# Laying the buffer pools of two graph layers over each other, and reloading a layer's values from another queue

## The chip, the cores and the metric

The kernel runs on one core of a Trainium2 chip. Its time is the device time of one launch in microseconds (us). A core has five engines with an instruction stream each: PE (TensorE), DVE (VectorE), ACT (ScalarE), POOL (GpSimd) and SP (SyncE, which here only issues DMAs). Each works through its stream in order; semaphores tie the streams together. Data lies in SBUF (128 partitions), matmul results in PSUM, everything else in DRAM.

## The reference

A graph of N = 2708 nodes with 256 features, and a sparse weighted adjacency matrix. Two residual layers, each followed by a layer norm:

```python
# layer 0, two steps
R = S + eye(N); R = R / R.sum(-1, keepdims=True)
Xf = Xa = X; Z = 0
for n in range(2):
    A = top_p_attention(Xa, W1, W2, W3)     # softmax rows, the largest entries up to 0.9 of the mass
    Xf = R @ Xf
    Xa = A @ Xa
    Z = Z + Xf @ U1[n].T + Xa @ U2[n].T
x = layernorm(x + layernorm(X + Z) * ln_g + ln_b)
# layer 1, four heads of 64
Wh  = einsum('nd,hdo->nho', x, W)
s_i = einsum('nho,ho->nh', Wh, a_src); s_j = einsum('nho,ho->nh', Wh, a_dst)
e   = leaky_relu(s_i[:, None, :] + s_j[None, :, :], 0.2)
e   = where(adj != 0 or i == j, e, -inf)
x   = layernorm(x + einsum('ijh,jho->iho', softmax(e, axis=1), Wh))
```

## The kernel before, in words

The nodes are cut into 22 tiles, 16 of 128 rows and 6 of 110. All arithmetic is in float32.

Layer 0 (`fast_layer0`) runs two steps of 22 attention tiles. For a tile it makes the scores `e` (128 x 2708), finds the kept entries on DVE, transposes `e` in pieces and multiplies it with the node values (`weigh`, tiles `tr`, `eT`, `att`). Beside that runs a second stream of matmuls, the walk with R (tiles `blk`, `walk`), and per tile a chain of small steps written as generators. The last chain, `finish`, adds the terms, takes two layer norms (BN statistics on DVE, `ln_ve` and `ln_rs` on POOL, the scaling on DVE at L906), writes the new features into `xe`, and then calls `sources`. The order inside layer 0 is written out by hand (`slot`, `step`, `doing`, inside `manual_schedule`); what stands outside of it is put in order by the framework's scheduler.

`sources` prepares layer 1 for a tile of nodes: it transposes the features (L141), copies them (`xT`, L143), multiplies them with the layer's weights (L147), and from the product makes on ACT the exponentials `sb` and `tj` (L151, L152), the source score `s_src` (L153) and the values times `sb` (`cs`, L157). The values go to DRAM, to `vd[t]` (L160, on SP's queue).

Layer 1 (`layer1`) takes the target nodes in three groups of 8, 8 and 6 tiles (1024, 1024 and 660 columns) and, for each group, all 22 source tiles `j`. Before a group, `targets` makes `r`, the targets' exponentials spread over all partitions: four transposes (`aux`, L1101) and one ACT exponential (L1105) for each of the group's tiles. For a source tile, `neighbours` loads a block of the adjacency matrix (`bar`, L1115, on SP's queue, four buffers), turns it into a 0/1 mask on ACT (sign L1116, square L1121), and in the blocks that hold the diagonal sets it on POOL in between (L1119, L1120). DVE then makes for each head `pt` = max(r, tj) x mask (L1168), and PE multiplies `pt` with the values `v[j]` (L1176, 8 matmuls of 512 columns) and with `bj[j]`, which is `sb` spread over 32 columns and gives the softmax denominator (L1183, 8 matmuls). The sums stay in six PSUM banks over the 22 source tiles. At the end of a group `settle` turns them back, divides, adds the residual, takes the layer norm and stores.

All the values are read back from DRAM at the start of layer 1, for the 22 tiles one after the other, by ACT's queue, and all `bj` are made there on POOL:

```python
for t in range(NT):
    m = rows[t]
    nc.scalar.dma_start(v[t][:m].rearrange("p h o -> p (h o)"), vd[t][:m])
    nc.gpsimd.tensor_copy(bj[t][:m], sb[:m, t, :].unsqueeze(2).to_broadcast([m, H, 32]))
```

SBUF and PSUM are handed out in pools that lie one after the other in the order in which they are opened. Layer 0 closes its pools before layer 1 opens its own, which therefore come to lie over the same addresses. Nothing makes the engines stop there: an instruction of layer 1 that writes a new tile waits on semaphores until the old users of what lies below have finished. So which pool lies over which decides when the first loads, masks and exponentials of layer 1 can start. In the kernel before, the four `bar` buffers and part of `r` lie over buffers that `finish` uses (`heldp`, `finp`).

After both layers a flag says whether the fast path's assumptions held; if not, `general_layer0` and `layer1` run again. With these inputs they don't.

Of the kernel before, what the change touches and what calls it, by code (L numbers as in the profile page):

```python
# [8 lines left out]
F32 = mybir.dt.float32  # L9
# [5 lines left out]
PSUM = bass.MemoryType.PSUM  # L15

P = 128
# [21 lines left out]
HELD = 8  # L39
# [6 lines left out]
def kernel(  # L46
# [16 lines left out]
    nc = tc.nc  # L63
    N, D = x.shape
    DA = w1T.shape[1]
    STEPS = u1T.shape[0]
    H, _, FO = gat_w.shape
    DC = D // P
    NT = (N + P - 1) // P
# [44 lines left out]
    vd = [kept.tile([P, D], F32, name=f"v_{t}") for t in range(NT)]  # L114
# [339 lines left out]
    def fast_layer0():  # L454

        l0 = ExitStack()
        w0 = l0.enter_context(tc.tile_pool(name="w0", bufs=1))
        rowp = l0.enter_context(tc.tile_pool(name="rowp", bufs=2))
        keep = l0.enter_context(tc.tile_pool(name="keep", bufs=1))
        HN = N // 2  # L460
        HT = NT // 2
        pieces = [(c, min(CHUNK, HN - c)) for c in range(0, HN, CHUNK)]
# [43 lines left out]
        nc.gpsimd.memset(wants, 0.0)  # L506
        nc.gpsimd.memset(haves, 0.0)

        qT = keep.tile([P, N], F32, name="qT")
        yw = keep.tile([P, NT, D], F32, name="yw")  # L510
        ba = keep.tile([P, NT, D], F32, name="ba")
        rinv = keep.tile([P, NT], F32, name="rinv")

        dram = l0.enter_context(tc.tile_pool(name="dram", bufs=1, space=bass.MemoryType.DRAM))
        c1 = [dram.tile([P, D], F32, name=f"c1_{t}") for t in range(NT)]
        c2 = [dram.tile([P, D], F32, name=f"c2_{t}") for t in range(NT)]

        sortp = l0.enter_context(tc.tile_pool(name="sortp", bufs=1))
        heldp = l0.enter_context(tc.tile_pool(name="heldp", bufs=HELD))
        finp = l0.enter_context(tc.tile_pool(name="finp", bufs=2))  # L520
        ep = l0.enter_context(tc.tile_pool(name="ep", bufs=3))
        wk = l0.enter_context(tc.tile_pool(name="wk", bufs=1))

        kT = [wk.tile([P, HN], F32, name="junk"), keep.tile([P, HN], F32, name="kT1")]
        tpp = l0.enter_context(tc.tile_pool(name="tpp", bufs=3))
        adjp = l0.enter_context(tc.tile_pool(name="adjp", bufs=3))
        ps_lg = l0.enter_context(tc.tile_pool(name="ps_lg", bufs=2, space=PSUM))
        ps_tr = l0.enter_context(tc.tile_pool(name="ps_tr", bufs=2, space=PSUM))
        ps_at = l0.enter_context(tc.tile_pool(name="ps_at", bufs=1, space=PSUM))
        ps_wk = l0.enter_context(tc.tile_pool(name="ps_wk", bufs=1, space=PSUM))  # L530


        tmp = ep.tile([P, N], F32, name="e")
# [534 lines left out]

    def layer1():
        l1 = ExitStack()  # L1070
        keep = l1.enter_context(tc.tile_pool(name="keep1", bufs=1))
        pp = l1.enter_context(tc.tile_pool(name="pp", bufs=2))
        GT = 8
        spans = [list(range(g, min(g + GT, NT))) for g in range(0, NT, GT)]
        GW = GT * rows[0]


        v = [keep.tile([P, H, FO], F32, name=f"v{t}") for t in range(NT)]
        bj = [keep.tile([P, H, 32], F32, name=f"bj{t}") for t in range(NT)]
        for t in range(NT):  # L1080
            m = rows[t]
            nc.scalar.dma_start(v[t][:m].rearrange("p h o -> p (h o)"), vd[t][:m])
            nc.gpsimd.tensor_copy(
                bj[t][:m], sb[:m, t, :].unsqueeze(2).to_broadcast([m, H, 32])
            )

        rp = l1.enter_context(tc.tile_pool(name="rp", bufs=2))
        adjp = l1.enter_context(tc.tile_pool(name="adjp1", bufs=4))
        pj = l1.enter_context(tc.tile_pool(name="pj", bufs=2))
        ps_v = l1.enter_context(tc.tile_pool(name="ps_v", bufs=1, space=PSUM))  # L1090
        ps_u = l1.enter_context(tc.tile_pool(name="ps_u", bufs=2, space=PSUM))

        def targets(g):

            r = rp.tile([P, H, GW], F32, name="r")
            i0 = off[spans[g][0]]
            for t in spans[g]:
                m = rows[t]
                tr = ps_u.tile([P, H, P], F32, name="aux")
                for h in range(H):  # L1100
                    nc.tensor.transpose(  # L1101
                        tr[:, h, :m], s_src[:m, t, h : h + 1].to_broadcast([m, P]),
                        ident[:m, :m],
                    )
                nc.scalar.activation(  # L1105
                    r[:, :, off[t] - i0 : off[t + 1] - i0], tr[:, :, :m], AF.Exp, scale=1.0 - NEG_SLOPE
                )
            return r

        def neighbours(g, j):  # L1110

            k = rows[j]
            i0, i1 = off[spans[g][0]], off[spans[g][-1] + 1]
            bar = adjp.tile([P, GW], F32, name="bar")[:k, : i1 - i0]
            nc.sync.dma_start(bar, adjT[off[j] : off[j + 1], i0:i1])  # L1115
            nc.scalar.activation(bar, bar, AF.Sign)  # L1116
            if j in spans[g]:
                own = bar[:, off[j] - i0 : off[j + 1] - i0]
                nc.gpsimd.tensor_mul(own, own, offdiag[:k, :k])  # L1119
                nc.gpsimd.tensor_add(own, own, ident[:k, :k])  # L1120
            nc.scalar.activation(bar, bar, AF.Square)  # L1121
            return bar
# [27 lines left out]
        for g, span in enumerate(spans):  # L1150
            gw = off[span[-1] + 1] - off[span[0]]
            cuts = [(c, min(CHUNK, gw - c)) for c in range(0, gw, CHUNK)]
            acc = [
                [ps_v.tile([P, CHUNK], F32, name=f"acc{k}_{c}") for c in range(len(cuts))]
                for k in range(3)
            ]
            for j in range(NT):
                k = rows[j]
                if j == 2 and due:
                    settle(*due)  # L1160
                if j == NT // 2 and g + 1 < len(spans):
                    r_next = targets(g + 1)
                mask = neighbours(g, j)
                at = dict(start=(j == 0), stop=(j == NT - 1), skip_group_check=True)
                pts = []
                for h in range(H):
                    pt = pj.tile([P, GW], F32, name=f"pt{h}")
                    nc.vector.scalar_tensor_tensor(  # L1168
                        pt[:k, :gw], r[:k, h, :gw], tj[:k, j, h : h + 1], mask,
                        op0=ALU.max, op1=ALU.mult,  # L1170
                    )
                    pts.append(pt)
                    if h % 2 == 1:
                        for c, (c0, w) in enumerate(cuts):
                            for q in range(2):
                                nc.tensor.matmul(  # L1176
                                    acc[h // 2][c][q * FO : (q + 1) * FO, :w],
                                    v[j][:k, h - 1 + q, :],
                                    pts[h - 1 + q][:k, c0 : c0 + w], **at,
                                )  # L1180
                for c, (c0, w) in enumerate(cuts):
                    for h in range(H):
                        nc.tensor.matmul(  # L1183
                            acc[2][c][h * 32 : (h + 1) * 32, :w],
                            bj[j][:k, h, :], pts[h][:k, c0 : c0 + w], **at,
                        )
            r = r_next
            val = pp.tile([P, 2, GW], F32, name="val")
            den = pp.tile([P, GW], F32, name="den")
            for c, (c0, w) in enumerate(cuts):  # L1190
                nc.scalar.copy(val[:, 0, c0 : c0 + w], acc[0][c][:, :w])
                nc.vector.tensor_copy(val[:, 1, c0 : c0 + w], acc[1][c][:, :w])
                nc.scalar.copy(den[:, c0 : c0 + w], acc[2][c][:, :w])
            due = (g, val, den)
        settle(*due)
        l1.close()

    fast_layer0()
    layer1()
    flag = nc.values_load(bad[0:1, 0:1])  # L1200
    with tc.If(flag > 0):
        general_layer0()
        layer1()
# [45 lines left out]
```

The softmax here doesn't subtract the row's maximum and nothing guards it: scores larger than these inputs give would overflow.

## Time and profile before

| | |
|---|---|
| time, median of 3 runs | 1722.71 us (1722.70 to 1722.73) |
| span of the profiled execution | 1720.4 us |
| PE busy | 1624.2 us (94%) |
| DVE busy | 1221.5 us (71%) |
| ACT busy | 771.1 us (45%) |
| POOL busy | 450.9 us (26%) |
| moved by DMA | 113.92 MB, mean 66 GB/s |
| end of layer 0's last layer norm to the first matmul of layer 1 | 1314.8 to 1336.2 us |

Busy times are sums over the whole span. "L1168" is line 1168 of the kernel. In the lists of waits, a row says which engine, at which line, stood idle until which other one had finished something, for how long in total, how often, and the longest; where an instruction waits for several others, the row names the one that came last by the profile. In the timelines, instructions of one line that follow each other are merged; "ACTq" and "SPq" are the parts of ACT and SP that issue DMAs.

### The profile page before, as it was taken

How to read it: one execution, taken by the hardware profiler on the slowest of the kernel's cores; microseconds unless marked ns; L12 is line 12 of the kernel's file. 1: busy time of each engine (PE TensorE's matmuls, PEld its weight loads, DVE VectorE, ACT ScalarE, POOL GpSimd, SP SyncE). 2: the span in 40 equal slices, each digit the busy share in tenths (PEclk: the TensorE clock that was granted, in tenths of full speed). 3: DMA queues.
4: the chain of work that ended last, by engine and by line, in shares of the span. 5: the costliest groups of instructions: out<-in, count | busy, mean ns of one | idle time of the engine just before them, and what ended most of it. 6: DMA issues, size and time to landing. Idle time of an engine off the chain costs nothing.

```text
span 1720.4 us, 24503 instructions
## 1 busy us (share of the span) xinstructions
PE 1624.2 (94%) x8434; PEld 1080.7 (63%) x8434; DVE 1221.5 (71%) x3681; ACT 771.1 (45%) x1345; POOL 450.9 (26%) x915
## 2 busy tenths in 40 slices
PE   5799999999999998999999999999995999999895
PEld 4577777777777776777787878777774332322332
DVE  2754555554555108888989999999891979888896
ACT  1233333333333236656676666766632544243241
POOL 0011111111111133322344444345433300440313
PEclk9899999999999999999999999999997999999998
DMA  6111011101111132212222233322213323232231
GB/s 162 33 45 45 26 42 43 42 24 43 42 39 42 41 104 65 62 48 70 78 81 81 68 84 84 84 56 72 73 39 115 95 83 92 86 97 77 73 84 32
DMA packets 153875, 113.92 MB, mean 66 GB/s; under 512 B 39898, under 2 KB 144094, under 8 KB 153742
## 3 DMA queue, kind: packets, MB, share of 16 engines
q1 hardware_dynamic: 145048, 101.88, 21.8%
q10 hardware_dynamic: 6582, 4.84, 1.0%
q0 software_dynamic: 2112, 5.55, 0.9%
q8 instruction: 68, 1.11, 0.3%
q14 instruction: 65, 0.53, 0.1%
HBM read 101.16 MB, written 11.09 MB: 65 GB/s over the span
## 4 chain that ended last, share of the span: by engine, by line
PE 70%; DVE 15%; ACT 6%; POOL 4%; DMA 2%; issue 2%; ACTq 0%; SPq 0%; POOLq 0%; DVEq 0%
PE att L187 20%; PE walk L816 16%; PE acc L1176 11%; PE acc L1183 6%; PE lg L591 4%; PE tr L172 3%; ACT e L595 3%; PE tr L559 2%; DVE cand L696 2%; PE tr L872 2%; PE tr L852 2%; DVE scr L762 2%; DVE e L765 1%; DVE scr L681 1%; DVE work L716 1%
## 5 line engine op out<-in xcount | busy, mean ns | idle before, releaser
L1168 DVE SCALAR_TENSOR_TENSOR pt<-r,tj,bar 128x1024 f32<-128x1024 f32 (+3 forms) x264 | 296.6, 1185 | 49.2 <-DMA v<-v 20.0
L616 ACT ACTIVATE junk<-e,minus,rth 128x2708 bf16<-128x2708 f32 (+1 forms) x88 | 232.8, 2646 | 33.5 <-POOL rth L648 32.7
L816 PE MATMUL walk<-xe,blk 128*128 128x257 f32 (+3 forms) x968 | 243.8, 385 | 0.0
L187 PE MATMUL att<-xe,eT 128*128 128x256 f32 (+3 forms) x968 | 233.4, 381 | 7.6 <-ACT eT L178 7.6
L187 PE MATMUL att<-ba,eT 128*128 128x256 f32 (+3 forms) x968 | 235.2, 384 | 5.0 <-ACT eT L178 5.0
L1176 PE MATMUL acc<-pt,v 128*64 128x512 f32 (+3 forms) x1056 | 229.8, 553 | 4.6 <-DVE pt L1168 4.6
L816 PE MATMUL walk<-yw,blk 128*128 128x256 f32 (+3 forms) x968 | 228.2, 381 | 1.7 <-ACT xw L886 1.7
L178 ACT COPY eT<-tr 128x512 f32<-128x512 f32 (+5 forms) x264 | 136.9, 536 | 193.8 <-PE tr L172 193.4
L816 PEld LDWEIGHTS walk<-xe,blk 128*128 128x128 f32 (+3 forms) x968 | 173.7, 187 | 64.9 <-issue 41.8
L816 PEld LDWEIGHTS walk<-yw,blk 128*128 128x128 f32 (+3 forms) x968 | 176.9, 186 | 42.2 <-issue 12.3
L696 DVE MAX8 cand<-e 128x8 f32<-128x170 f32 (+1 forms) x352 | 89.4, 323 | 146.8 <-ACT e L595 146.8
L187 PEld LDWEIGHTS att<-ba,eT 128*128 128x128 f32 (+3 forms) x968 | 172.6, 188 | 33.4 <-ACT eT L178 10.2
L187 PEld LDWEIGHTS att<-xe,eT 128*128 128x128 f32 (+3 forms) x968 | 171.0, 186 | 35.7 <-ACT eT L178 12.6
L595 ACT ACTIVATE e<-lg 128x1024 f32<-128x1024 f32 (+1 forms) x132 | 121.0, 921 | 133.3 <-PE lg L591 128.4
L1176 PEld LDWEIGHTS acc<-pt,v 128*64 128x64 f32 (+1 forms) x1056 | 73.6, 137 | 153.9 <-issue 110.5
L172 PE MATMUL tr<-ident,e 128*128 128x128 f32 (+3 forms) x968 | 139.0, 270 | 6.1 <-DVE e L765 4.9
L172 PEld LDWEIGHTS tr<-ident,e 128*128 128x128 f32 (+3 forms) x968 | 116.4, 139 | 30.9 <-issue 5.7
L1116 ACT ACTIVATE bar<-bar 128x1024 f32<-128x1024 f32 (+3 forms) x66 | 62.9, 955 | 144.7 <-DMA bar<-in_adjT_dram 127.6
L1183 PE MATMUL acc<-pt,bj 128*32 128x512 f32 (+3 forms) x1056 | 124.6, 549 | 0.0
L829 DVE TENSOR_TENSOR xf<-walk,xe 128x257 f32<-128x257 f32 (+1 forms) x22 | 9.4, 426 | 156.9 <-PE walk L816 156.9
L696 DVE MAX8 cand<-scr 128x8 f32<-128x97 f32 (+1 forms) x616 | 101.7, 244 | 0.0
L714 DVE MAX8 top<-work 128x8 f32<-128x128 f32 (+3 forms) x242 | 82.4, 340 | 8.3
(194 smaller groups left out, 2009.6 us busy)
## 6 DMA issues: line engine op xcount, KB each, us to landing
blk<-in_adjT_dram SPq DMA_DIRECT2D x32, 704.0 KB
bar<-in_adjT_dram SPq DMA_DIRECT2D x32, 512.0 KB
blk<-in_adjT_dram SPq DMA_DIRECT2D x32, 330.0 KB
blk<-in_adjT_dram SPq DMA_DIRECT2D x32, 320.0 KB
blk<-in_adjT_dram SPq DMA_DIRECT2D x12, 605.0 KB
bar<-in_adjT_dram SPq DMA_DIRECT2D x12, 440.0 KB
bar<-in_adjT_dram SPq DMA_DIRECT2D x16, 330.0 KB
c<-cs POOLq DMA_DIRECT2D x32, 128.0 KB, 2.9
```

What stands on the lines that cost most here:

```text
L172: nc.tensor.transpose(tr[: rows[t], q, :m], e[:m, off[t] : off[t + 1]], ident[:m, :m])
L178: copy(eT[:k, : len(grp), :m], tr[:k, : len(grp), :m])
L187: nc.tensor.matmul(acc, eT[: rows[t], q, :m], value(t), start=(t == 0), stop=(t == NT - 1),)
L591: nc.tensor.matmul(lg[:m, h, :w], qT[part, cols], kT[s][part, c0 : c0 + w], start=True, stop=True,)
L595: nc.scalar.activation(halves[:m, :, c0 : c0 + w], lg[:m, :, :w], AF.Exp, accum_out=zp[:m, n : n + 1],)
L616: nc.scalar.activation(junk[:m], e[:m], func, scale=rth, bias=minus1[:m], accum_out=acc)
L696: nc.vector.max(cand[:, n, :], src[:m, n * size : min(N, (n + 1) * size)])
L714: nc.vector.max(top[:, k : k + 8], work if k else flat)
L816: nc.tensor.matmul(ac[:m, :w], blk[: rows[j], j - j0, :m], cur[: rows[j], j, 0:w], start=(j == 0), stop=(j == NT - 1),)
L1168: nc.vector.scalar_tensor_tensor(pt[:k, :gw], r[:k, h, :gw], tj[:k, j, h : h + 1], mask, op0=ALU.max, op1=ALU.mult,)
L1176: nc.tensor.matmul(acc[h // 2][c][q * FO : (q + 1) * FO, :w], v[j][:k, h - 1 + q, :], pts[h - 1 + q][:k, c0 : c0 + w], **at,)
L1183: nc.tensor.matmul(acc[2][c][h * 32 : (h + 1) * 32, :w], bj[j][:k, h, :], pts[h][:k, c0 : c0 + w], **at,)
```

## The change

In both layers all pools are opened together, in another order, so that other pools lie over each other; the number and the size of the buffers stay as they are. In layer 0 the order is now `heldp`, `finp`, `rowp`, `w0`, `keep`, `sortp`, `adjp`, `ep`, `tpp`, `wk`, and in PSUM `ps_lg`, `ps_wk`, `ps_at`, `ps_tr`; in layer 1 it is `pp`, `keep1`, `pj`, `adjp1`, `rp`, and `ps_u`, `ps_v`. By this `pp` (results of a whole group) lies over `heldp`, `finp` and `rowp`; `keep1` (`v`, `bj`, allotted from tile 21 down to tile 0) lies over the last 64 bytes of `rowp`, over `w0` and over part of `keep`; `pj` (`pt`) lies over `keep` (`yw`, `ba`, `qT`); `adjp1` (`bar`) lies over `keep` (`qT`, `kT1`), `sortp` and the first 4 kB of `adjp`; and `rp` (`r`) over `adjp` and `ep`.

The reload of `v[j]` and the making of `bj[j]` move from the start of layer 1 into the loop of the first group: they are called one source tile at a time, ahead of that tile's adjacency load. The load is issued from SP's queue instead of ACT's.

```diff
--- before.py
+++ after.py
@@ -454,9 +454,18 @@
     def fast_layer0():
 
         l0 = ExitStack()
-        w0 = l0.enter_context(tc.tile_pool(name="w0", bufs=1))
-        rowp = l0.enter_context(tc.tile_pool(name="rowp", bufs=2))
-        keep = l0.enter_context(tc.tile_pool(name="keep", bufs=1))
+
+        heldp, finp, rowp, w0, keep, sortp, adjp, ep, tpp, wk = (
+            l0.enter_context(tc.tile_pool(name=name, bufs=bufs))
+            for name, bufs in (
+                ("heldp", HELD), ("finp", 2), ("rowp", 2), ("w0", 1), ("keep", 1),
+                ("sortp", 1), ("adjp", 3), ("ep", 3), ("tpp", 3), ("wk", 1),
+            )
+        )
+        ps_lg, ps_wk, ps_at, ps_tr = (
+            l0.enter_context(tc.tile_pool(name=name, bufs=bufs, space=PSUM))
+            for name, bufs in (("ps_lg", 2), ("ps_wk", 1), ("ps_at", 1), ("ps_tr", 2))
+        )
         HN = N // 2
         HT = NT // 2
         pieces = [(c, min(CHUNK, HN - c)) for c in range(0, HN, CHUNK)]
@@ -506,28 +515,17 @@
         nc.gpsimd.memset(wants, 0.0)
         nc.gpsimd.memset(haves, 0.0)
 
-        qT = keep.tile([P, N], F32, name="qT")
         yw = keep.tile([P, NT, D], F32, name="yw")
         ba = keep.tile([P, NT, D], F32, name="ba")
         rinv = keep.tile([P, NT], F32, name="rinv")
+        qT = keep.tile([P, N], F32, name="qT")
 
         dram = l0.enter_context(tc.tile_pool(name="dram", bufs=1, space=bass.MemoryType.DRAM))
         c1 = [dram.tile([P, D], F32, name=f"c1_{t}") for t in range(NT)]
         c2 = [dram.tile([P, D], F32, name=f"c2_{t}") for t in range(NT)]
 
-        sortp = l0.enter_context(tc.tile_pool(name="sortp", bufs=1))
-        heldp = l0.enter_context(tc.tile_pool(name="heldp", bufs=HELD))
-        finp = l0.enter_context(tc.tile_pool(name="finp", bufs=2))
-        ep = l0.enter_context(tc.tile_pool(name="ep", bufs=3))
-        wk = l0.enter_context(tc.tile_pool(name="wk", bufs=1))
 
         kT = [wk.tile([P, HN], F32, name="junk"), keep.tile([P, HN], F32, name="kT1")]
-        tpp = l0.enter_context(tc.tile_pool(name="tpp", bufs=3))
-        adjp = l0.enter_context(tc.tile_pool(name="adjp", bufs=3))
-        ps_lg = l0.enter_context(tc.tile_pool(name="ps_lg", bufs=2, space=PSUM))
-        ps_tr = l0.enter_context(tc.tile_pool(name="ps_tr", bufs=2, space=PSUM))
-        ps_at = l0.enter_context(tc.tile_pool(name="ps_at", bufs=1, space=PSUM))
-        ps_wk = l0.enter_context(tc.tile_pool(name="ps_wk", bufs=1, space=PSUM))
 
 
         tmp = ep.tile([P, N], F32, name="e")
@@ -1068,27 +1066,29 @@
 
     def layer1():
         l1 = ExitStack()
-        keep = l1.enter_context(tc.tile_pool(name="keep1", bufs=1))
-        pp = l1.enter_context(tc.tile_pool(name="pp", bufs=2))
+
+        pp, keep, pj, adjp, rp = (
+            l1.enter_context(tc.tile_pool(name=name, bufs=bufs))
+            for name, bufs in (("pp", 2), ("keep1", 1), ("pj", 2), ("adjp1", 4), ("rp", 2))
+        )
+        ps_u = l1.enter_context(tc.tile_pool(name="ps_u", bufs=2, space=PSUM))
+        ps_v = l1.enter_context(tc.tile_pool(name="ps_v", bufs=1, space=PSUM))
         GT = 8
         spans = [list(range(g, min(g + GT, NT))) for g in range(0, NT, GT)]
         GW = GT * rows[0]
 
 
-        v = [keep.tile([P, H, FO], F32, name=f"v{t}") for t in range(NT)]
-        bj = [keep.tile([P, H, 32], F32, name=f"bj{t}") for t in range(NT)]
-        for t in range(NT):
+        v, bj = {}, {}
+        for t in reversed(range(NT)):
+            v[t] = keep.tile([P, H, FO], F32, name=f"v{t}")
+            bj[t] = keep.tile([P, H, 32], F32, name=f"bj{t}")
+
+        def stationary(t):
             m = rows[t]
-            nc.scalar.dma_start(v[t][:m].rearrange("p h o -> p (h o)"), vd[t][:m])
+            nc.sync.dma_start(v[t][:m].rearrange("p h o -> p (h o)"), vd[t][:m])
             nc.gpsimd.tensor_copy(
                 bj[t][:m], sb[:m, t, :].unsqueeze(2).to_broadcast([m, H, 32])
             )
-
-        rp = l1.enter_context(tc.tile_pool(name="rp", bufs=2))
-        adjp = l1.enter_context(tc.tile_pool(name="adjp1", bufs=4))
-        pj = l1.enter_context(tc.tile_pool(name="pj", bufs=2))
-        ps_v = l1.enter_context(tc.tile_pool(name="ps_v", bufs=1, space=PSUM))
-        ps_u = l1.enter_context(tc.tile_pool(name="ps_u", bufs=2, space=PSUM))
 
         def targets(g):
 
@@ -1160,6 +1160,8 @@
                     settle(*due)
                 if j == NT // 2 and g + 1 < len(spans):
                     r_next = targets(g + 1)
+                if g == 0:
+                    stationary(j)
                 mask = neighbours(g, j)
                 at = dict(start=(j == 0), stop=(j == NT - 1), skip_group_check=True)
                 pts = []
```

## The prediction

> **What bounds the kernel now.** I read the busy time by stretches first, because the diff touches the end of layer 0 and the start of layer 1 only. Columns: busy us of PE, weight loads, DVE, ACT, POOL (instructions in brackets), granted clock, DMA share, GB/s.
>
> ```profile
> 1000.00:1280.00 280.00, 276.67 (x1379) 218.22 (x1378) 261.64 (x986) 178.12 (x310) 122.93 (x267) 1.00 0.28 72
> 1280.00:1300.00 20.00, 17.03 (x83) 13.43 (x82) 13.13 (x34) 4.85 (x15) 8.62 (x10) 0.91 0.02 6
> 1300.00:1320.00 20.00, 13.86 (x60) 9.68 (x59) 3.61 (x10) 7.74 (x37) 7.96 (x14) 0.74 0.22 67
> 1320.00:1340.00 20.00, 8.00 (x32) 4.71 (x33) 5.17 (x4) 7.24 (x10) 10.02 (x28) 0.66 0.64 201
> 1340.00:1470.00 130.00, 130.00 (x764) 37.25 (x762) 117.03 (x97) 57.63 (x61) 10.33 (x11) 1.00 0.31 91
> ```
>
> PE is busy in 277 of 280 us before the seam and in 130 of 130 after it. Between 1300 and 1340 it is busy 22 of 40 us, partly at half clock, and no engine is full: a seam of latencies. The waits there name them:
>
> ```profile
> DVE pt L1168 <- DMA v<-v: 20.0, 1, 20.0
> ...
> PE aux L1101 <- ACT r L1105: 11.2, 2, 10.4
> ...
> ACT r L1105 <- DMA v<-v: 10.5, 1, 10.5
> ```
>
> and SP's own waits there:
>
> ```profile
> SPq L1115 <- DVE xe L906: 7.0, 1, 7.0
> ```
>
> ACT in order of time shows why:
>
> ```profile
> 1318.36 0.93 ACT L157 ACTIVATE cs<-tr,sb 110x64 f32<-110x64 f32 x4
> 1319.16 1.19 ACT L1105 ACTIVATE r<-aux 128x512 f32<-128x512 f32 x2
> 1320.25 1.05 ACT L1116 ACTIVATE bar<-bar 128x1024 f32<-128x1024 f32 x1
> 1321.19 1.07 ACT L1105 ACTIVATE r<-aux 128x512 f32<-128x512 f32 x2
> 1321.90 10.82 ACTq L1082 DMA_DIRECT2D v<-v  x22
> 1332.77 1.09 ACT L1105 ACTIVATE r<-aux 128x512 f32<-128x512 f32 x2 [10.50 <-DMA v<-v]
> 1333.73 1.06 ACT L1121 ACTIVATE bar<-bar 128x1024 f32<-128x1024 f32 x1
> ```
>
> ACT spends 10.82 us issuing 22 loads of v, between six of the eight pieces of r and the last two; the first mask (L1121) stands behind these. DVE's first pt (1334.83) needs both, so its wait "on v" is really on ACT. The bar loads waited for the last layernorm (L906), with r's first piece (1315.83) right after it. PE:
>
> ```profile
> 1336.17 6.21 PE L1176 MATMUL acc<-pt,v 128*64 128x512 f32 x16 [0.78 <-DVE pt L1168]
> 1342.31 1.92 PE L1183 MATMUL acc<-pt,bj 128*32 128x512 f32 x16
> 1344.16 3.65 PE L1176 MATMUL acc<-pt,v 128*64 128x512 f32 x16
> ```
>
> The first source tile takes 1336.17 to 1344.16, slowed by pt and the half clock; later tiles come every 5.44 us (1344.16, 1349.60), DVE needing 4 x 1.30 = 5.2. From 1344.16 the pace is PE's, so the end moves by what the end of the first source tile moves.
>
> **What the Trainium skill says.** "TensorE: Matmul & The Clock Gate", Part 1 (the HAM clock gate): about 3.4 us idle halves PE's clock, about 3.4 us of activity restores it. The trace agrees: after an idle 4.26 us the clock is 0.50 over 1310 to 1318; it is 0.51 over 1326 to 1340 and 1.00 from 1340. "DMA: Bandwidth & Descriptors", Issuing engines are not separate DMA queues: DMAs of all engines share the 16 DMA engines; choosing the issuer saves only issue time. The trace fits: 298 GB/s over 1318 to 1326, issued by SP and ACT together. Same page, Anatomy of one DMA: about 2 us fixed, most of it waiting for the write to be confirmed; here the last v took 2.47 us on the chain. "GPSIMD Engine Reference", Specifications: POOL shares its SBUF interfaces with DVE; here L1120 takes 0.45 us alone, 1.32 with pt running.
>
> **The change, part by part.** The built order: DVE's is identical; PE, ACT, POOL and SP differ only from the last attention tile to the first source tiles. Layer 0 before that is unchanged, and I cost its new addresses at nothing; the trace can't show that, so I allow 1 us each way. Instruction counts are equal, but for bookkeeping: the 22 loads of v go from ACT to SP, nothing else is added or removed.
>
> *Placement.* r now lies over e and blk: its first piece waits for the last e and blk instead of the last layernorm. The four bars lie over qT, kT1 and e's neighbours: bar 0 waits for the last attention matmul, which ended at 1304.33 (1301.58 + 2.75), against an issue at 1314.87. Bars 0 and 1 are issued at about 1304.4 and move 1.05 MB; over 1316 to 1320 the DMAs moved 250 to 281 GB/s, so 4 us, and 2 more to land: 1310.5. Bars 2 and 3 stand on SP behind the store of tile 19 (about 1307.8), landing by 1315. None is then waited for.
>
> *What this puts in the way.* I walk the last two tiles, 20 and 21, through layernorm and `sources`. Four pieces of r go ahead of tile 20, hidden in its layernorm (PE idle 4.26 us at 1307). On POOL the diagonal fix of bar 0 (L1119, 0.45) fits the 0.76 us gap before tile 21's ln_ve, and L1120 follows ln_rs (done 1314.35): 1314.8. ACT's L1121 of bar 0 waits for it and holds ACT to 1315.8, where tile 20's sb started at 1314.60: +1.2. Then 1.15 us of sb to cs, xT of tile 21 at 1316.9 (was 1315.61), L147 from 1317.3, 2.1 us at half clock, to 1319.4. In that time ACT does two pieces of r (to 1318.3) and L1116 of bar 1 (to 1319.3). sb to cs of tile 21 end at 1320.6: the last v store goes out 1.35 us late, at 1320.65. It lands after 2.5 (at most 2.6 in before: store at 1319.31, first load, which waits for it, at 1321.90): 1323.1.
>
> *v on SP.* Loads are 0.29 to 0.62 us of issue each. v0 waits for the last store to land, since its pool touches rowp by 64 bytes; queued behind it on SP are v1 to v4 and bar 4. v0: 1323.1 + 0.4 + 2.5 = 1326.0. bar 4 leaves at about 1325, also needing bar 0's buffer (pt of tile 0 done 1323.6), lands by 1330 with v in the same engines, and its mask takes 1.05 + 0.5 + 1.32 + 1.06 = 3.9 more: 1334. DVE needs it after tile 3, about 1344. The later v (8 to 21) stand behind bars 5 and 6, which wait for pt of tiles 1 and 2; v8 is wanted at 1332.8 + 7 x 5.44 = 1371. SP's 22 x 0.4 = 9 us are hidden by these margins of 10 us and more.
>
> *bj on POOL.* bj0 waits for the same store, but also stands behind the fixes of bars 1 and 2. L1116 of bar 1 at 1319.3, + 1.8 on POOL = 1321.1, L1121 to 1322.1, L1116 of bar 2 to 1323.1, + 1.9 on POOL = 1325.0, bj0 0.23 (5.14 over 22) to 0.6 with DVE: 1325.5. The other 21 are wanted one per 5.44 us.
>
> *DVE, PE.* pt waits for the last r: 1318.4, four end at 1323.6. In the new PE order the first tile's eight bj products go first, then v. Start 1325.5; 1.85 + 3.58 = 5.43 us of work. At full clock, tile 0's share ends at 1331.0 (bj done 1327.3, v0 there since 1326.0). PE idles from about 1320.5, though, so I expect half clock for some 3.6 us, which loses 1.8: 1332.8. Against 1344.16 that gains 13.2 or 11.4; I take the middle, 12.3.
>
> *Sum.* 1720.4 - 12.3 = 1708.1 us of span. The unprofiled runs stand at 1722.71, 2.3 above that span (1722.70 to 1722.73): 1710.4. As parts: the 10.5 us of ACT and some 10 us of waiting for layernorm before bar and r are removed; the last store, its landing, POOL's queue and the load of v0 give about 8 back.
>
> Bounds for what before doesn't show: the landing of the store 2.0 to 3.0, of v0 2.0 to 3.5 beside bar 4; bj0 0.23 to 0.7; POOL's L1120 0.45 or 1.32; the half clock 0 to 2.5 us; tile 21's L147 1.0 or 2.1. All good: bj0 at 1323.5, v0 at 1325, full clock, 1329.2, gain 15. All bad: bj0 at 1327, v0 at 1328, half clock, 1335, gain 9.
>
> **Rivals.**
> *Shorter tail* (gain 14 to 17, 1706 to 1708.7): the transposes for r keep PE warm and POOL runs its fixes at 0.45. For it: PE gets work in the idle 1307 to 1311. Against: five idle us remain before the first product.
> *A new wait takes over* (gain 4 to 9, 1713.7 to 1718.7): the 64-byte touch makes bj0 and v0 queue on POOL and SP, and mask fixes slow down beside pt. For it: L1120 is at 1.32 in five of six. Against: nothing there is longer than 2 us.
> *No change* (1719.3 to 1726.1): layer 1 is paced by the bar loads, so an early start is given back. Against: PE 130.00 of 130.
> *Slower*: SP is blocked by the loads of v, each held until the DMA eight before it on the same semaphore has landed. At 2.5 us of SP each instead of 0.4, the 22 ahead of bar 7 end at 1323 + 55 = 1378, and its mask is ready 9 us later, at 1387; tile 7 wants it at 1332.8 + 6 x 5.44 = 1365. That loses 22 against 12 gained: 1722.7 + 10 = 1733. It decides from about 2 us per load (1323 + 22 x 2.05 + 9 = 1377, 12 late). Against: ACT issued them at 0.49 under the same rotation.
> That the pools don't free the loads early is excluded by the built waits.
>
> **How the numbers follow.** Forecast (1708.7 to 1711.7) 0.58, shorter tail 0.17, new wait 0.19, no change 0.03, slower 0.03. 0.2% (3.4 us) is about what a measurement of this kernel can tell from no change. The range 1706.8 to 1713.9 takes the forecast, most of the shorter tail and the edge of the new wait.
>
> **What would show it.** After: L1116 of bar 0 near 1309; last L160 at 1320 to 1321; first pt near 1318; first PE product at 1325 to 1326 with bj, at half clock; tile 1 done at 5.44 after tile 0; no wait of DVE on bar before tile 8. Wrong if PE's waits in layer 1 name DMA, if the first product comes after 1328, or if the stretch before 1280 has changed in length.

## The result, and the profile after

The changed kernel takes 1712.72 us (median of 4 runs, 1711.16 to 1714.42) beside 1722.70 for the kernel before on the same chip (1720.45 to 1722.73): a ratio of 0.9945, 95% interval 0.9928 to 0.9963. On a second chip it was 1711.85 against 1720.97, 0.9948 (0.9934 to 0.9962). The forecast was 1710.4 with a range of 1706.8 to 1713.9. The profiled execution has a span of 1711.1 us, 9.3 less than before.

Busy time by stretches, the columns as in the prediction (PE, weight loads, DVE, ACT, POOL, clock, DMA share, GB/s):

```profile
1000.00:1280.00 280.00, 276.89 (x1382) 218.35 (x1381) 261.63 (x983) 178.49 (x312) 123.22 (x267) 1.00 0.28 72
1280.00:1300.00 20.00, 17.22 (x85) 13.51 (x84) 13.54 (x35) 4.85 (x15) 8.66 (x10) 0.91 0.02 6
1300.00:1320.00 20.00, 15.35 (x80) 11.73 (x78) 5.08 (x12) 12.40 (x43) 9.23 (x17) 0.83 0.37 123
1320.00:1340.00 20.00, 13.09 (x64) 3.56 (x64) 15.80 (x11) 9.50 (x13) 15.46 (x32) 0.83 0.53 158
1340.00:1460.00 120.00, 120.00 (x707) 34.17 (x706) 105.14 (x89) 50.65 (x53) 2.93 (x5) 1.00 0.33 96
```

Up to 1300 no row differs by more than 0.5 us on any engine. Between 1300 and 1340 PE is busy 28.4 of 40 us, where it was 21.9, and it is again full behind that. The list of waits of 1284 to 1345 no longer has DVE, PE or ACT waiting for v. What releases the first product is now POOL (engine, line, waited for: us in total, times, longest):

```profile
ACT bar L1121 <- POOL bar L1120: 12.0, 6, 4.4
...
PEld acc L1185 <- POOL bj L1089: 8.2, 2, 7.5
...
PE acc L1185 <- POOL bj L1089: 7.3, 1, 7.3
```

PE in order of time (start, us, engine, line; in brackets the idle time before and what ended it):

```profile
1318.60 1.04 PE L1101 MATMUL aux<-ident,s_src 128*128 128x128 f32 x8
1326.91 4.50 PE L1185 MATMUL acc<-pt,bj 128*32 128x512 f32 x18 [7.28 <-POOL bj L1089]
1331.34 7.09 PE L1178 MATMUL acc<-pt,v 128*64 128x512 f32 x32
1338.35 1.92 PE L1185 MATMUL acc<-pt,bj 128*32 128x512 f32 x14
1340.20 3.65 PE L1178 MATMUL acc<-pt,v 128*64 128x512 f32 x16
```

The products of source tiles 0 and 1 are interleaved and end at 1340.20, where in before they ended at 1349.60; from there on tiles follow each other at 5.44 us (1345.64, 1351.08), as before. A product is listed as two passes: the first 18 of `bj` take 4.43 us until the next line starts, while 16 take 1.85 us later. Two things are in this, and the weight loads tell them apart (first the start of layer 1, then an undisturbed tile):

```profile
1326.91 0.20 PEld L1185 LDWEIGHTS acc<-pt,bj 128*32 128x32 f32 x8 [7.52 <-POOL bj L1089]
1327.77 0.20 PEld L1185 LDWEIGHTS acc<-pt,bj 128*32 128x32 f32 x4 [0.66 <-issue]
1328.62 0.20 PEld L1185 LDWEIGHTS acc<-pt,bj 128*32 128x32 f32 x4 [0.66 <-issue]
1329.47 0.18 PEld L1185 LDWEIGHTS acc<-pt,bj 128*32 128x32 f32 x1 [0.66 <-POOL bj L1089]
1330.33 0.17 PEld L1185 LDWEIGHTS acc<-pt,bj 128*32 128x32 f32 x1 [0.68 <-issue]
1331.33 0.20 PEld L1178 LDWEIGHTS acc<-pt,v 128*64 128x64 f32 x4 [0.84 <-issue]
...
1343.78 0.16 PEld L1185 LDWEIGHTS acc<-pt,bj 128*32 128x32 f32 x8 [0.81 <-issue]
1344.24 0.13 PEld L1185 LDWEIGHTS acc<-pt,bj 128*32 128x32 f32 x4 [0.30 <-issue]
1344.67 0.13 PEld L1185 LDWEIGHTS acc<-pt,bj 128*32 128x32 f32 x4 [0.30 <-issue]
```

In both, the four heads go in step: weights are loaded in fours, one round of passes ahead. The rounds follow each other at 0.43 us in the undisturbed tile and at 0.85 us here, where the granted clock is 0.50 (from 1323.7 to 1330.3; 1.00 from 1330.5 on). So the first 16 passes, the eight products of tile 0, take 3.42 us (1326.91 to 1330.33) instead of 1.85, and the half clock costs about 1.6 us. The other two passes are a ninth product, which belongs to tile 1. It goes alone, takes 1.0 us, and saves nothing later: the 14 passes that are left of tile 1 take 1.85 us, as 16 do. This order costs about 0.8 us (1.0, less 0.15 that the `v` products of both tiles save by standing together). The two add up: tiles 0 and 1 take 13.29 us from the first product on, and two undisturbed tiles take 10.88.

And what lies ahead of the first product, from the timeline of all engines between 1323 and 1328:

```profile
1323.84 5.32 DVE L1170 SCALAR_TENSOR_TENSOR pt<-r,tj,bar 128x1024 f32<-128x1024 f32 x4
1324.31 1.31 POOL L1120 TENSOR_TENSOR bar<-bar,ident 128x128 f32<-128x128 f32 x1
...
1325.57 2.51 POOL L1089 COPY bj<-sb 128x128 f32<-128x128 f32 x2
```

DVE has been making pt since 1318.65 and is on its second tile. POOL is still setting the diagonal of tile 2's mask, and makes `bj[0]` only then.

Executions differ in layer 0: over the eleven traces the first matmul starts between 12.9 and 14.3 us, and layer 0's last product (the check sum, `walk<-ones,total`) between 1301.5 and 1304.9; two traces of the changed kernel itself have it at 1304.89 and 1303.81. So that this doesn't blur a seam of ten microseconds, all traces are compared by the distance from that product to the start of PE's first product of layer 1, and to the end of source tile 2, after which the pace is about 5.44 us a tile in all of them:

| kernel | first product, us | end of tile 2, us | time / before | 95% |
|---|---|---|---|---|
| before | 31.7 | 50.6 | 1 | |
| after | 22.0 | 40.8 | 0.9945 | 0.9928 to 0.9963 |
| after, second chip | 22.1 | 40.6 | 0.9948 | 0.9934 to 0.9962 |
| placement alone | 22.0 | 41.8 | 0.9961 | 0.9947 to 0.9974 |
| reload alone | 23.9 | 43.8 | 0.9969 | 0.9957 to 0.9981 |
| after, v loaded by ACT | 22.1 | 40.6 | 0.9949 | 0.9936 to 0.9963 |
| after, twelve extra products | 25.0 | 41.3 | 0.9948 | 0.9934 to 0.9961 |
| after, eight extra products | 21.4 | 37.7 | 0.9933 | 0.9919 to 0.9946 |
| after, bj on ACT | 20.0 | 39.6 | 0.9938 | 0.9924 to 0.9952 |
| after, gap | 19.2 | 37.3 | 0.9931 | 0.9917 to 0.9944 |
| after, gap and bj on ACT | 16.1 | 35.6 | 0.9915 | 0.9902 to 0.9929 |

For after: first product 1326.91 - 1304.89 = 22.0; end of tile 2 1345.64 - 1304.89 = 40.8; for before 1336.17 - 1304.45 and 1355.04 - 1304.45. The seam is 9.8 us shorter.

### The profile page after: what moved, and what is told of

Read it like the earlier page. It is cut to its first block, busy times and chain, and to the rows that moved or that the text cites. A ratio compares the mean times of both kernels' runs of the same rounds, so it can differ in the third digit from the quotient of the medians.

```text
span 1711.1 us, 24516 instructions
## 1 busy us (share of the span) xinstructions
PE 1620.7 (95%) x8434; PEld 1077.5 (63%) x8434; DVE 1222.7 (71%) x3681; ACT 770.7 (45%) x1345; POOL 449.9 (26%) x915
## 4 chain that ended last, share of the span: by engine, by line
PE 70%; DVE 15%; ACT 6%; POOL 4%; issue 2%; DMA 2%; ACTq 0%; POOLq 0%; DVEq 0%; SPq 0%
PE att L187 20%; PE walk L814 16%; PE acc L1178 11%; PE acc L1185 6%; PE lg L589 4%; PE tr L172 3%; ACT e L593 3%; PE tr L557 2%; DVE cand L694 2%; PE tr L870 2%; PE tr L850 2%; DVE scr L760 2%; DVE e L763 1%; DVE scr L679 1%; DVE work L714 1%
## 5 line engine op out<-in xcount | busy, mean ns | idle before, releaser
L814 PEld LDWEIGHTS walk<-xe,blk 128*128 128x128 f32 (+3 forms) x968 | 173.7, 187 | 64.9 <-issue 41.8
L814 PEld LDWEIGHTS walk<-yw,blk 128*128 128x128 f32 (+3 forms) x968 | 176.9, 186 | 42.5 <-issue 12.3
L1116 ACT ACTIVATE bar<-bar 128x1024 f32<-128x1024 f32 (+3 forms) x66 | 63.0, 956 | 150.5 <-DMA bar<-in_adjT_dram 141.2
```

The lines of the kernel that those rows point to most:

```text
L814: nc.tensor.matmul(ac[:m, :w], blk[: rows[j], j - j0, :m], cur[: rows[j], j, 0:w], start=(j == 0), stop=(j == NT - 1),)
```

## The experiments

My theory going in: two things held layer 1 back, ACT's block of 22 issues and the wait of `bar` and `r` for the last layer norm; with both gone, a third chain (last store of v, the touch with `rowp`, POOL's order, `bj[0]`) and PE's half clock keep some 5 us. Rivals: one of the two edits is the whole gain; SP's queue as such is what helps or limits; neither the touch nor the clock matters.

**The placement alone.** After's pools, loads and copies all at the head of layer 1, the loads on ACT:

```diff
-        def stationary(t):
+        for t in range(NT):
             m = rows[t]
-            nc.sync.dma_start(v[t][:m].rearrange("p h o -> p (h o)"), vd[t][:m])
+            nc.scalar.dma_start(v[t][:m].rearrange("p h o -> p (h o)"), vd[t][:m])
...
-                if g == 0:
-                    stationary(j)
```

> The pools of after, with the 22 loads of v on ACT's queue and the 22 copies of bj at the head of layer 1, as before. Theory (two starts had to come forward, r and the masks on one side and bj and v on the other, and after both edits the chain from the last store through bj to the first product sets the end): the loads now stand behind all of r and the first masks on ACT, so they no longer delay the first pt, and bj 0 waits for the last store as in after; the first product stays near 1327 and the time at 1713 (1711 to 1716). Rival, the reload is the whole gain (22 issues at 0.49 us on ACT): they still hold ACT for 10.8 us, so 1720 to 1723. Rival, the 22 bj copies ahead of the mask of tile 3 on POOL at 0.74 us each become the wait: 1714 to 1718.

Measured: 1713.83 us against 1720.48, ratio 0.9961. The first product comes exactly where after has it (22.0). ACT and DVE show where the block of issues went:

```profile
1322.02 12.07 ACTq L1088 DMA_DIRECT2D v<-v  x19
1334.19 2.00 ACT L1121 ACTIVATE bar<-bar 128x1024 f32<-128x1024 f32 x2 [11.43 <-DMA v<-v]
```

```profile
1335.28 11.86 DVE L1168 SCALAR_TENSOR_TENSOR pt<-r,tj,bar 128x1024 f32<-128x1024 f32 x9 [7.99 <-ACT bar L1121]
```

In the new order the block stands behind all of `r` and the masks of tiles 0 and 1. It still holds ACT for 12 us, but only tile 2's mask waits for it, and tile 2 ends a microsecond later than in after (41.8 against 40.8). PE is not idle there, but DVE makes tile 2's last pt only by 1340.56, and in PE's order one product of `bj` goes alone ahead of the second half of `v`:

```profile
1340.14 1.04 PE L1183 MATMUL acc<-pt,bj 128*32 128x512 f32 x2
1341.12 1.94 PE L1176 MATMUL acc<-pt,v 128*64 128x512 f32 x8
```

This product takes 0.98 us alone, at the full clock, which supports the reading of the ninth product in after. So the reload is not the whole gain: placement alone brings 8.8 of the 9.8 us.

**The reload alone.** Before's pools, and `stationary(j)` per source tile on SP:

```diff
-        for t in range(NT):
+        def stationary(t):
             m = rows[t]
-            nc.scalar.dma_start(v[t][:m].rearrange("p h o -> p (h o)"), vd[t][:m])
+            nc.sync.dma_start(v[t][:m].rearrange("p h o -> p (h o)"), vd[t][:m])
...
+                if g == 0:
+                    stationary(j)
```

> The pools of before, with v loaded on SP one source tile at a time. Theory: ACT is free of 10.8 us of issues, so the first pt moves from 1334.8 to about 1324 and tiles 0 and 1 end about 10 us earlier than in before; r and the masks still wait for the last layernorm, so DVE does not run ahead: 1713 (1710 to 1717). Rival, the placement is the whole gain: 1720 to 1723. Rival, the bj copies, which stand ahead of the mask of tile 1 on POOL in this order and run beside pt, hold tile 1: 1715 to 1719.

Measured: 1714.64 us against 1720.48, ratio 0.9969; the seam is 6.8 us shorter. pt starts at 1324.04, 10.8 us earlier than in before, as expected from ACT's block; but 20.2 us after layer 0's last product, where after has 13.8. POOL and ACT:

```profile
1321.82 7.21 POOL L1083 COPY bj<-sb 128x128 f32<-128x128 f32 x22
```

```profile
1330.88 1.06 ACT L1121 ACTIVATE bar<-bar 128x1024 f32<-128x1024 f32 x1 [5.05 <-POOL bar L1120]
```

The 22 copies run as one block on POOL here, and tile 1's mask waits 5 us for it, as the rival with the copies had it. (Tiles 0 and 1 were expected to end about 10 us earlier than in before; they end 6.8 earlier.) The block also slows DVE. The timeline of all engines in the 1.4 us from 1325.6:

```profile
1324.04 3.62 DVE L1170 SCALAR_TENSOR_TENSOR pt<-r,tj,bar 128x1024 f32<-128x1024 f32 x1 [9.82 <-DMA v<-v]
...
1325.52 2.29 POOL L1083 COPY bj<-sb 110x128 f32<-110x128 f32 x5
```

The first pt takes 3.62 us beside these copies, where one takes 1.30 otherwise, and ends at 1327.66; the first product follows at 1327.76. Without the 2.3 us more that this pt took it would have stood at 21.6 after layer 0's last product, ahead of after's 22.0. (The wait of pt put down to v ended when ACT's square of the mask did, at 1322.97, and the last `r`, at 1323.9.) Of the 3.0 us that this kernel lacks against after, 1.9 are the later start, for which the copies are enough. The rest comes behind it: the clock is 0.50 for 5.3 us from the first product on, against 3.5 in after, and here too a product of `bj` goes alone, ahead of `v`.

The two edits bring 8.8 and 6.8 us alone and 9.8 together. They don't add because each only brings forward a part of what the first product has to wait for, and another part is then the last. In after and in placement alone it is `bj[0]`, which starts 20.7 us after layer 0's last product in both; in reload alone the copies start at 18.0, and the first pt is the last.

**SP's queue.** After, with one word changed:

```diff
-            nc.sync.dma_start(v[t][:m].rearrange("p h o -> p (h o)"), vd[t][:m])
+            nc.scalar.dma_start(v[t][:m].rearrange("p h o -> p (h o)"), vd[t][:m])
```

> After, with the loads of v still one source tile at a time, but on ACT's queue. Theory (what mattered is that they no longer stand in one block ahead of the masks, not whose queue they are on): an issue costs ACT 0.49 us, 22 of them 10.8 us spread over the first 10 tiles, in which ACT has time; within 1.5 us of after. Rival (SP's queue as such is the gain): the first load waits for the last store on ACT and holds the masks of tiles 1 to 3, so 4 us or more above after.

Measured: 1712.55 us beside 1711.85 for after on the same chip, both against 1720.97 (0.9949 and 0.9948); the end of tile 2 is at 40.6 in both. Spread over the tiles, the issues cost ACT nothing that anyone waits for:

```profile
1329.61 1.50 ACTq L1088 DMA_DIRECT2D v<-v  x3
1330.57 1.04 ACT L1116 ACTIVATE bar<-bar 128x1024 f32<-128x1024 f32 x1
1337.06 1.06 ACT L1121 ACTIVATE bar<-bar 128x1024 f32<-128x1024 f32 x1 [5.46 <-POOL bar L1120]
1337.07 1.29 ACTq L1088 DMA_DIRECT2D v<-v  x3
```

It is the block that was costly, not the queue.

After itself ran beside this kernel and the next two, as the mark to compare with.

> The changed kernel itself, beside the variants on the same chip. Every theory: 0.9945 of before (0.993 to 0.996), about 1711.5 where before is 1721; tile 2 ends 40.9 us after the last attention product. Whether its runs scatter by 3 us again is open.

It met it, with runs from 1711.2 to 1713.37. Of the 1.4 us between the spans of its two traces (1711.1 and 1709.7), 1.1 are there when layer 0 ends.

**The half clock, first try.** After, with products whose result nothing reads, placed between the transposes of `r` and the first product:

```diff
         r = targets(0)
+        warm = ps_u.tile([P, H, P], F32, name="aux").rearrange("p h o -> p (h o)")
+        for _ in range(12):
+            nc.tensor.matmul(warm, ident, r[:, 0, 0:CHUNK], start=True, stop=True)
```

> After, with twelve extra products of the identity with r into a spare PSUM tile that nothing reads, after the transposes of r, in the time in which PE waits for bj 0 (1319 to 1327). Theory: the clock is granted in full when the first products come, so the nine bj products of tile 0 take 2.1 us and not 4.4, and the time falls by about 2.3 us: 1710.4 (1709.5 to 1711.5), and the runs lie closer together than the 3.3 us of after. Rival, the slow first products are not a matter of the clock, or other work beside them sets their pace: no change within 0.7 us.

Measured: 1711.27 us against 1720.48, ratio 0.9948: no different from after, and my sizing was wrong.

```profile
1318.05 10.46 PE L1151 MATMUL aux<-r,ident 128*128 128x512 f32 x24
1328.45 3.65 PE L1181 MATMUL acc<-pt,v 128*64 128x512 f32 x16
1332.03 1.92 PE L1188 MATMUL acc<-pt,bj 128*32 128x512 f32 x16
```

The clock was full, and tile 0 took 5.44 us from its first product on; but the twelve products took 0.87 us each, 10.4 us together, for a gap that in after is 7.3 us long, and the first product came 3.0 us later than in after. What was gained behind it, this length took. The run tells neither way.

**The half clock, second try.** Eight instead of twelve.

> As the kernel with twelve extra products, with eight of them (0.87 us each in that run, so 7.0 us, from 1318.1 to 1325.1 on its scale, before bj 0 is there). Theory (half clock costs the first products about 2.3 us): the first product comes where after has it, at the full clock, and tile 2 ends 38.5 us after the last attention product instead of 40.9; the time is 1.5 to 2.5 us below after. Rival: the clock falls again in the gap of some 1.5 us, or the first products are held by pt or v, and it is within 0.7 us of after.

Measured: 1709.17 us (0.9933), beside 1711.85 for after (0.9948). PE's timeline, and PE's clock in the 20 us from 1316 (the third number from the end):

```profile
1315.95 7.03 PE L1151 MATMUL aux<-r,ident 128*128 128x512 f32 x16
1322.91 3.65 PE L1181 MATMUL acc<-pt,v 128*64 128x512 f32 x16
1326.49 1.92 PE L1188 MATMUL acc<-pt,bj 128*32 128x512 f32 x16
```

```profile
1316.00:1336.00 20.00, 20.00 (x93) 6.54 (x93) 16.95 (x14) 7.24 (x14) 17.56 (x27) 1.00 0.65 203
```

From 1316 on PE is never idle and never at half clock; the first product comes at 21.4 instead of 22.0, tile 2 ends at 37.7 instead of 40.6 to 40.8. Of the 2.8 to 3.0 us gained, 0.6 are the earlier start. The other 2.2 to 2.4 are not the clock alone: PE's order is another here too, all of a tile's `v` and then all of its `bj`, so that no product goes alone. By the weight loads shown above, the half clock is about 1.6 us of it and the order about 0.8; no run changed the order alone. (After's second trace has the same order and 0.4 us less at half clock, and loses 2.2 us where the first loses 2.4.) The two intervals of the time overlap; the difference shows in the traces.

**The 64 bytes.** After, with an unused pool between `pp` and `keep1`, so that `v` and `bj` no longer lie over the end of `rowp`:

```diff
-        pp, keep, pj, adjp, rp = (
+        pp, gap, keep, pj, adjp, rp = (
...
-            for name, bufs in (("pp", 2), ("keep1", 1), ("pj", 2), ("adjp1", 4), ("rp", 2))
+            for name, bufs in (
+                ("pp", 2), ("gap", 1), ("keep1", 1), ("pj", 2), ("adjp1", 4), ("rp", 2)
+            )
...
+        nc.vector.memset(gap.tile([P, 32], F32, name="gap"), 0.0)
```

> After, with one unused pool of 128 bytes a row between pp and keep1, so that v and bj no longer touch the two last layernorm rows of layer 0 (64 bytes in after). Theory: bj 0 and the first loads of v then wait for nothing of the last stores, POOL's queue is not held, and the first product follows the first pt at about 1320.5 instead of 1326.9; DVE (5.26 us a tile) and PE (5.44) then run from there, so 4 to 8 us below after: 1707 (1705 to 1709). Rival, the load of v on SP's queue is what holds the first products: within 2 us of after, 1711 to 1713. Rival, the half clock of PE eats the gain: 2 to 4 us below after.

Measured: 1708.68 us against 1720.48, ratio 0.9931; the seam is 3.4 us shorter than after's. The touch was worth that much, but less than the 4 to 8 us expected. The gain is of the size that the rival with the half clock named, but not for its reason: the clock is 1.00 from 1322 on, and the first product starts at 1323.18. PE then follows DVE, and tiles 0 to 2 take 18.2 us instead of 16.3. But the first product had been expected near 1320.5, and what made it late stands on POOL and DVE, at the last layer norm of layer 0:

```profile
1314.24 0.29 POOL L1092 COPY bj<-sb 128x128 f32<-128x128 f32 x1
1314.49 0.57 POOL L901 TENSOR_TENSOR ln_rs<-ln_ve,minus_half 110x1 f32<-110x1 f32 x1
1315.03 0.46 POOL L1123 TENSOR_TENSOR bar<-bar,ident 128x128 f32<-128x128 f32 x1
1315.42 3.50 POOL L1092 COPY bj<-sb 128x128 f32<-128x128 f32 x14
```

```profile
1315.10 2.73 DVE L904 TENSOR_SCALAR xe<-hh,ln_mv,ln_rs 110x256 f32<-110x256 f32 x1 [2.12 <-POOL ln_rs L901]
```

Freed of their wait, the copies of `bj` moved ahead in POOL's order: seven of them in front of the last layer norm's `ln_rs`, fourteen beside the write of `xe` that follows it. `ln_rs` came 1.1 us later than in after (10.5 against 9.3 us after layer 0's last product), and the write took 2.73 us where it took 0.54; the last layer norm ended at 13.8 instead of 10.5. A wait had been holding back work that did harm.

**The gap, and bj on ACT.** In the kernel with the gap:

```diff
-            nc.gpsimd.tensor_copy(
+            nc.scalar.copy(
                 bj[t][:m], sb[:m, t, :].unsqueeze(2).to_broadcast([m, H, 32])
```

> The kernel with the gap, with the 22 copies of bj on ACT instead of POOL. In the gap kernel 20 copies ran on POOL ahead of the last layernorm's reciprocal root and beside DVE's last write of xe, which took 2.73 us and not 0.54, so the last layernorm ended 13.9 us after the last attention product instead of 10.6. Theory: with POOL free the last layernorm is back at 10.6, the first pt at 13.9 instead of 17.1, and the time 2.5 to 4 us below the gap kernel: 1705.5 (1704.5 to 1707) where before is 1720.5. Rival: ACT, which now has 22 copies between the masks, holds the masks, and it is within 1 us of the gap kernel or above it.

Measured: 1706.84 us (1704.45 to 1707.11) against 1720.97, ratio 0.9915. The last layer norm ends 10.5 us after layer 0's last product again, the first pt comes at 14.5 and the first product at 16.1:

```profile
1318.31 2.92 PE L1181 MATMUL acc<-pt,v 128*64 128x512 f32 x8 [0.43 <-ACT bj L1092]
```

The seam is 1.7 us shorter than with the gap alone (35.6 against 37.3), less than the 3.1 by which the first product comes earlier, and less than the 2.5 to 4 of the theory. The clock is full here too (1.00 from 1318.3 on), and PE is not idle after its first product, but it follows DVE: tiles 0 and 1 take it 7.55 and 6.56 us, with a product of `bj` alone in each (0.98 us). In tile 1 DVE had waited for the mask (a gap of 1.44 us ahead of its pt), whose sign ACT does only after the last `sources`. What each of these is worth was not tried. This kernel beats both the kernel before and after: its interval, 0.9902 to 0.9929, lies below after's, 0.9934 to 0.9962.

**bj on ACT without the gap.** The same edit on after: the touch stays, POOL's queue and its slow copy go.

> After, without the gap, with the 22 copies of bj on ACT instead of POOL. On POOL bj 0 started 20.7 us after layer 0's last product and took 0.74 us, behind the diagonal of tile 2's mask, although the first load of v, which waits for the same last store, was issued 3.0 us earlier. Theory (POOL's order and its slow copy, not the store, release the first product in after): on ACT bj 0 stands behind the signs of masks 2 and 3 (done 19.7 after that product) and takes 0.3, so the first product comes 20.2 us after layer 0's last product instead of 22.0, still at half clock, and tile 2 ends 1.5 us earlier: 1 to 2 us below after, 0.9938 of before. Rival (the landing of the last store is what it waits for): first product within 0.5 us of 22.0, no change.

Measured: 1709.89 us against 1720.59, ratio 0.9938; first product at 20.0, tile 2 ends at 39.6, 1.1 us earlier than in after.

```profile
1320.22 1.99 ACT L1116 ACTIVATE bar<-bar 128x1024 f32<-128x1024 f32 x2
1322.11 0.68 ACT L1089 COPY bj<-sb 128x128 f32<-128x128 f32 x3
```

The three copies take 0.68 us here, and PE's first weight load follows the first of them:

```profile
1322.44 0.18 PEld L1185 LDWEIGHTS acc<-pt,bj 128*32 128x32 f32 x2 [4.55 <-ACT bj L1089]
```

So in after it was POOL's order and its copy that released the first product, not the landing of the last store. (The 0.74 us in the expectation is a mean over six copies; `bj[0]` itself took 1.28, see below.) Of the 2.0 us of earlier start 1.1 are left at tile 2: the clock is at half for the first 4.9 us of products, 3.5 in after, and a product of `bj` goes alone at this clock (1322.45 to 1324.29).

## Why the prediction was right, and where it was 2 us off

The direction, the place and most of the steps came true; the gain was put at 12.3 us and is 9.8 in the seam.

- *Placement.* L1116 of bar 0 started at 1308.71 ("near 1309"), the first pt at 1318.65 ("near 1318"). The experiment with the placement alone shows that this edit carries most of the gain.
- *What this puts in the way.* The last store was put at 1320.65; SP issued it by 1320.86. The walk through tiles 20 and 21 held, with layer 0 ending 0.44 us later in this execution (1304.89 against 1304.45).
- *v on SP.* v0 was never waited for, and no load of v was. The other queue made no difference.
- *bj on POOL.* The start of `bj[0]` was put at 1325.0 and was 1325.57, which is the 0.44 us and 0.13 more. Its length was put at 0.23 to 0.6, with 0.7 as the bound, and this term failed: two copies took 2.51 us, the longest 1.28. The first product came at 1326.91 instead of 1325.5, outside the 1325 to 1326 of the prediction; 0.44 of it is layer 0, about 1.0 is POOL: 0.1 its later start, the rest the copy. I had the same effect in front of me in before, where L1120 takes 0.45 us alone and 1.32 beside pt, and didn't apply it to the copy.
- *DVE, PE.* The half clock was put at some 3.6 us and a loss of 1.8, and then the middle between half and full was taken, 0.9. It was there for 3.5 us of products and cost about 1.6, so the case was sized rightly and the middle was the mistake: the middle of two cases is a time that neither gives, and the trace of before already had 0.50 after a shorter idle time. A second part was put at nothing: the prediction has PE's order as tile 0's eight `bj` products and then `v`. The ninth product, of tile 1, stands between them, and costs about 0.8.
- *Sum.* 12.3, less 0.7 for taking the middle, less 0.8 for the ninth product, less 1.0 for POOL, makes 9.8. The whole shortfall lies in the last two terms of the sum.
- *Layer 0 unchanged* was costed at nothing. The stretch from 1000 to 1280 has PE busy 276.89 us where it had 276.67. Nothing speaks against it: the nine traces with the new addresses end layer 0 at 1301.5 to 1304.9, the two with the old ones at 1303.9 and 1304.5. But a microsecond either way would not be seen in this scatter.

The rivals: *shorter tail* did not happen: the clock was at half when the first products came. Of the variants, only the gap with `bj` on ACT gains as much in the seam as this rival named (15.0 us). *A new wait takes over* had the right mechanism (the touch, POOL's queue, slow work beside pt), and that mechanism was part of the forecast's own sum; its range began at 1713.7, 1.0 above what was measured. The measured time lies between the forecast's own range, which ended at 1711.7, and this rival's. *No change* is refuted by PE 120.00 of 120 from 1340 on. *Slower* needed 2 us per load of v on SP; the trace has five in 2.24 us and seven in 2.90.

Open: which part of layer 0 makes the executions differ by 3 us; 1.4 of it is there at the first matmul, and the rest was not followed. The times follow the seam within their intervals, but gain up to 2 us less than it in most variants (placement alone: seam -8.8, time -6.7 of 1720.5). A part of this lies behind the seam: from the end of tile 2 to the end of the span most traces, before and after among them, take 365.2 to 365.5 us, but placement alone takes 366.9, and the kernels with eight and twelve extra products take 366.8 and 366.2. Why is not known.

## What to carry to other kernels

Where one stage hands over to the next, follow every input of the first instruction of the new stage back to its last release, and sum each chain: removing the longest one brings only the distance to the next, and two edits that each remove a chain don't add. Price a small copy on POOL at what it costs beside DVE's work at that moment, and the first matmuls at half clock where PE has been idle for some microseconds before (3.1 to 7.3 in the traces that had it). Look in PE's order for narrow products that stand alone. And look at what a wait was holding back before taking it away: without it the scheduler may place the freed work ahead of something that matters.

## What the runs showed of the hardware that I had not expected

- A copy of 128x128 on POOL takes 0.23 us while DVE does nothing (22 in 5.14, in before) and up to 1.28 beside pt. The harm goes both ways: beside a row of copies that kept nearly their full pace (14 in 3.50) DVE's write of 110x256 took 2.73 us instead of 0.54, and beside another such row a pt took 3.62 instead of 1.30.
- The same copy takes 0.2 us on ACT beside pt (3 in 0.68 us), and pt hardly suffers: eight took 10.86 us there and 10.51 in after.
- Products with few stationary columns share the time only with neighbours for other columns. With 512 columns moving, 128 stationary columns take 0.44 us a pass (24 in 10.46); 64 take 0.23 (16 in 3.65) and 32 take 0.116 (16 in 1.85) where two or four heads go in step. A product of 32 columns alone took 0.98 us for its two passes, no less than one over the full width, and seven took as long as eight. Extra products meant to keep PE busy have to be priced by the full width.
- From the first product on, the half clock lasted 3.5 us in one trace of the changed kernel, 3.1 in the other and 5.3 in reload alone, so its price is not the same in every execution.
